# Two buffers in turn for the rows of the first attention's bias table

## The chip, the cores and the metric

The kernel runs on one core of one Trainium2 chip, as one launch. The metric is the device time of that launch in microseconds, and less is better. Five runs of the kernel before have a median of 1389.54 us (1382.15 to 1393.66).

## The reference, cut to what matters

The reference is a chain of four layers, each a half step of a feed-forward block, an attention, and another half step of feed-forward. The change lies in the first attention, whose scores get a bias that depends only on how far query and key lie apart, per head:

```python
x = x + 0.5 * _L0_ffn_ref(_layernorm(x, axis=-1), ...)
x = x + _L0_attn_ref(_layernorm(x, axis=-1), ..., L0_attn_rel_pos_emb)

# in _L0_attn_ref: x is (4, 512, 128), 16 heads of 8
att = jnp.einsum('bhtd,bhsd->bhts', q, k) / np.sqrt(D)
table = rel_pos_emb.reshape(2 * MAX_LEN - 1, H, D).sum(axis=-1)
pos = jnp.arange(T)
rel_idx = pos[:, None] - pos[None, :] + (MAX_LEN - 1)
bias = jnp.transpose(table[rel_idx], (2, 0, 1))
att = att + bias[None]
att = jnp.where(pos[None, :] > pos[:, None], -jnp.inf, att)
```

MAX_LEN is 128 and an index beyond the table is clamped to its last row, so a key more than 127 places back gets one constant per head.

## The kernel before, in words

Everything is 32-bit floating point. The 2048 tokens lie in four batches of 512 (`xs[b]`, 128 partitions by four tiles of 128). The first feed-forward is a mixture of eight experts, the class `Mixture`. Its method `experts` loops over the experts: `fetch` reads an expert's tokens from DRAM (`d_f<-disp_f`, L788), `prepare` transposes them (L807), then PE multiplies them by the two weights (L831, L867), VectorE adds the bias (L847), ScalarE weighs (L852), and GpSimd scatters the rows to a DRAM tensor `res_f` with indirect DMAs (L853). The last of these scatters ends the mixture.

The first attention, `l0_attn` (L1621), begins per batch with `combine` (L877): a read of that batch's rows of `res_f` (`r_f<-res_f`, L882, issued by SP), the addition to `xs[b]` (L883), a norm (L191 to L209), and PE's transposes (`T_a`, L218), from which queries, keys and values are made (L1535, L1463, L1396). Each score tile on VectorE then adds the bias table (`sc_a<-s_a,table`, L998 and L1002).

The table is made by the generator `prep_table` (L1553), whose steps are called in between other work. One row of 384 numbers per head (zeros, 128 biases, minus 1e30) goes to DRAM as `rows` (`tab_rows`, L1575). `fetch(h)` (L1581) reads for two heads the rows that are shifted by one element from partition to partition (`rev<-tab_rows`, 256 KB, L1583). A product with the matrix `flip` on PE (L1596, two passes of 128x512 each) turns the order of the partitions, and ScalarE copies the product into the table (`table<-turned`, L1597). There are 16 heads, hence eight reads, eight products and eight copies, named here by their first head: 0, 2, ... 14.

`behind_expert` (L2579) hands the steps out. The first reads are traced beside the fourth expert; the products and the other reads are traced after all eight experts (`whole(made)`, L2592) and ahead of `l0_attn`. The tile `rev` has the tag `raw` in the pool `stage`, which has five buffers for that tag. The same five serve other short-lived tiles, among them the raw weights that `load_T` reads (L166), so also those of the second layer (`prep_l1`, L1658: `raw_gate1T`, `raw_wg1T`, `raw_wu1T`, `raw_sg1T`, `raw_su1T`).

What sets the order: a planner that builds the program gives each engine and each DMA queue a static order and inserts the waits. Inside some stretches (`manual_schedule`) the order on the compute engines is that of the source; the stretch of the first attention is one (L1314: PE, VectorE, ScalarE, GpSimd, not SP). The experts and the table's products lie outside of them, and SP's queue of DMAs there is the planner's. A DMA in SP's queue that waits holds up those behind it.

## Time and profile before

| | |
|---|---|
| median of five runs | 1389.54 us |
| profiled execution, its own time | 1394.12 us |
| its span | 1392.4 us |
| mean granted clock of TensorE | 0.912 |
| PE busy | 1182.6 us (85%) |
| VectorE, ScalarE, GpSimd busy | 63%, 50%, 50% |
| products with `flip` on PE (L1596) | 92.7 to 100.8 us, 16 passes |
| reads `rev<-tab_rows` (L1583) | eight, issued 54.5 to 95.6 us |
| first use of the table on VectorE (L1002) | 116.6 us |

Times inside the execution count from the start of the span. PE is TensorE's matmuls, PEld its weight loads, DVE VectorE, ACT ScalarE, POOL GpSimd, and SPq the instructions with which SP issues DMAs. In a timeline a line gives start, duration, engine, line of the kernel, operation, output and inputs, and how many instructions are merged; the bracket at its end is the time that the engine sat idle before it, and what ended that. In the chain that ended last, a line gives start, duration and what held the chain in that time.

### The profile page before, as it was taken

To read this page: it belongs to the slowest core of one execution; us is meant where nothing else is said; L and a number is where in the kernel's file an instruction comes from. 1 tells how busy PE (TensorE), PEld (TensorE's weight loads), DVE (VectorE), ACT (ScalarE), POOL (GpSimd) and SP (SyncE) were. 2 spreads that over 40 slices of the span, in tenths; PEclk is the share of its full clock that TensorE was granted. 3 is DMA by queue.
4 is the path that set the end of the run, shared out by engine and by line. 5 is a ranking of instruction groups with operands and counts; after the bars stand their busy time and mean duration, and the time that the engine had idled before them with its cause. 6 is when DMAs were issued, how large, how long until landed. Compare 5 with 4: busy or idle time off the path is not lost.

```text
span 1392.4 us, 27536 instructions
## 1 busy us (share of the span) xinstructions
PE 1182.6 (85%) x9665; PEld 765.8 (55%) x9665; DVE 877.1 (63%) x3269; ACT 691.9 (50%) x1481; POOL 694.5 (50%) x786
## 2 busy tenths in 40 slices
PE   5787999996999999998989897649599999898494
PEld 4554776775766666666755453437354444343272
DVE  5236878772366557776549999724286787783253
ACT  3244977883443367776732221114236766565132
POOL 5545878882534767876624243344432334212253
PEclk9997999997999999999999997669778999998697
DMA  8533433203425584341039200032133313100334
GB/s 272 179 86 105 126 97 102 72 6 94 145 63 132 163 281 145 93 133 60 2 68 329 92 16 16 16 98 79 53 99 114 107 41 97 46 16 16 85 92 113
DMA packets 116649, 137.60 MB, mean 99 GB/s; under 512 B 11160, under 2 KB 68744, under 8 KB 116512
## 3 DMA queue, kind: packets, MB, share of 16 engines
q1 hardware_dynamic: 107456, 121.05, 29.1%
q0 software_dynamic: 6656, 13.22, 2.9%
q10 hardware_dynamic: 2400, 1.57, 0.4%
q8 instruction: 77, 1.26, 0.4%
q14 instruction: 60, 0.49, 0.1%
HBM read 78.22 MB, written 57.58 MB: 98 GB/s over the span
## 4 chain that ended last, share of the span: by engine, by line
PE 54%; DVE 22%; issue 9%; POOL 6%; DMA 5%; ACT 3%; another core or an unknown queue 1%; SPq 0%; POOLq 0%; DVEq 0%; ACTq 0%
PE t_a L1026 9%; PE s_a L968 6%; PE h_f L831 5%; PE acc_a L1048 5%; PE o_f L867 5%; PE acc_a L1215 4%; DVE top_a L1073 3%; DVE x L2279 3%; POOL res_f L853 2%; PE ot_a L1268 2%; PE t_a L968 2%; DVE sc_a L1002 1%; PE t_a L1103 1%; DVE sc_a L998 1%; DMA d_f<-disp_f 1%
## 5 line engine op out<-in xcount | busy, mean ns | idle before, releaser
L1013 POOL TENSOR_SCALAR sc_a<-sc_a,top_a 128x128 f32<-128x128 f32 (+3 forms) x256 | 275.9, 1093 | 74.2 <-DVE top_a L998 48.1
L968 PE MATMUL s_a<-k_a,q_a 32*128 32x512 f32 (+3 forms) x1040 | 183.3, 488 | 20.7 <-DVE top_a L1073 7.6
L1026 PE MATMUL t_a<-ident,sc_a 128*128 128x128 f32 x1280 | 174.3, 284 | 8.1 <-DVE top_a L1002 7.7
L1073 DVE TENSOR_REDUCE top_a<-s_a 128x1 f32<-128x512 f32 x240 | 150.9, 682 | 40.7 <-PE t_a L1103 18.6
L853 POOL DMA_INDIRECT res_f<-y_f,back_f x112 | 107.1, 956 | 127.2 <-ACT y_f L852 90.1
L1109 ACT ACTIVATE w_a<-t_a 128x512 f32<-128x512 f32 x240 | 127.8, 600 | 74.1 <-PE t_a L1103 39.6
L1026 PEld LDWEIGHTS t_a<-ident,sc_a 128*128 128x128 f32 x1280 | 145.8, 145 | 33.5 <-issue 12.6
L1015 ACT ACTIVATE sc_a<-sc_a,top_a 128x128 f32<-128x128 f32 (+3 forms) x256 | 134.2, 576 | 14.5 <-DVE top_a L1002 10.3
L1035 ACT ACTIVATE w_a<-t_a 128x256 f32<-128x256 f32 (+2 forms) x192 | 95.0, 528 | 64.4 <-PE t_a L1026 63.2
L968 PEld LDWEIGHTS s_a<-k_a,q_a 32*128 32x128 f32 x1040 | 79.5, 190 | 72.8 <-issue 26.3
L867 PE MATMUL o_f<-w_l,h_f 128*128 128x128 f32 (+1 forms) x896 | 110.6, 278 | 1.4 <-ACT h_f L835 0.9
L831 PE MATMUL h_f<-dT_f,w_l 128*128 128x320 f32 (+1 forms) x256 | 106.7, 555 | 2.6 <-ACT dT_f L809 2.6
L867 PEld LDWEIGHTS o_f<-w_l,h_f 128*128 128x128 f32 (+1 forms) x896 | 102.4, 184 | 10.4 <-DVE back_f L816 3.9
L1048 PE MATMUL acc_a<-w_a,vpad 128*32 128x128 f32 x2560 | 98.8, 280 | 0.6 <-ACT w_a L1035 0.6
L1037 ACT COPY w_a<-t_a 128x256 f32<-128x256 f32 (+2 forms) x192 | 93.6, 526 | 8.1 <-PE t_a L1026 7.8
L1002 DVE CUSTOM_DVE_ANT_0 sc_a<-s_a,future 128x128 f32<-128x128 f32 (+3 forms) x128 | 62.3, 487 | 49.0 <-PE s_a L968 40.8
L852 ACT ACTIVATE y_f<-o_f,d_f 128x128 f32<-128x128 f32 (+1 forms) x112 | 39.0, 394 | 102.7 <-DVE o_f L847 90.4
L1215 PE MATMUL acc_a<-w_a,vpad 128*32 128x256 f32 x1024 | 87.7, 413 | 2.4 <-ACT w_a L1109 2.3
L1048 PEld LDWEIGHTS acc_a<-w_a,vpad 128*32 128x32 f32 x2560 | 63.4, 110 | 23.5 <-issue 18.2
L968 PE MATMUL t_a<-q_a,k_a 32*128 32x512 f32 x240 | 73.4, 516 | 1.1 <-DVE top_a L1073 0.5
L836 DVE TENSOR_SCALAR h_f<-h_f,b1T_l 128x320 f32<-128x320 f32 (+1 forms) x64 | 41.4, 650 | 51.9 <-PE h_f L831 47.4
L807 PE MATMUL dT_f<-ident,d_f 128*128 128x128 f32 (+1 forms) x112 | 21.2, 296 | 58.3 <-DMA d_f<-disp_f 39.8
(607 smaller groups left out, 2297.9 us busy)
## 6 DMA issues: line engine op xcount, KB each, us to landing
fac_a<-fac_a_sb SPq DMA_DIRECT2D x36, 256.0 KB
d_f<-disp_f SPq DMA_DIRECT2D x32, 260.0 KB
w_l<-in_L_ffn_w_dram SPq DMA_DIRECT2D x16, 512.0 KB
cb_f<-rows_f SPq DMA_DIRECT2D x16, 512.0 KB
q_a<-fac_a SPq DMA_DIRECT2D x32, 256.0 KB
k_a<-fac_a SPq DMA_DIRECT2D x32, 256.0 KB
disp_f<-zeros_f SPq DMA_DIRECT2D x4, 2048.0 KB
q_a<-qrows_a SPq DMA_DIRECT2D x30, 256.0 KB
```

Source lines behind the costliest of these rows:

```text
L831: nc.tensor.matmul(ps[u][:, :cap], w1[:, e, (c + u) * P : (c + u + 1) * P], dT, start=True, stop=True)
L853: nc.gpsimd.indirect_dma_start(out=self.back[e * per + s][:, :], out_offset=bass.IndirectOffsetOnAxis(ap=back[:m, s : s + 1], axis=0), in_ ...
L867: nc.tensor.matmul(po[:m, s, :], h[:, c, s * P : s * P + m], w2[:, e, c, :], start=(c == 0), stop=(c == NC - 1),)
L968: nc.tensor.matmul(ps[:, n0:n1], q[r : r + SLOT, i * P : (i + 1) * P].bitcast(as_), k[r : r + SLOT, n0:n1].bitcast(as_), start=True, stop= ...
L1013: nc.gpsimd.tensor_scalar(sc, sc, top, None, ALU.subtract)
L1015: nc.scalar.activation(sc, sc, AF.Exp, bias=top, scale=-1.0)
L1026: nc.tensor.transpose(ps[:, x * n + j * P : x * n + (j + 1) * P], st["sc", u, i, r0 + x][:, j * P : (j + 1) * P], ident,)
L1035: nc.scalar.activation(w[:, :m], ps[:, :m], AF.Exp)
L1048: nc.tensor.matmul(st["acc", u][r * SLOT : (r + 1) * SLOT, i * P : (i + 1) * P], vpads[b % 2][:, j, g * 4 + r, :], st["w", u, i, r][:, j * ...
L1073: nc.vector.tensor_reduce(st["top", u][:, i, r : r + 1], ps, AX.X, ALU.max, negate=True)
L1109: nc.scalar.activation(w, st["t", u, j, r], AF.Exp)
L1215: nc.tensor.matmul(acc[r * SLOT : (r + 1) * SLOT, n0:n1], vpads[b % 2][:, j, g * 4 + r, :], st["w", u, j, r, half] if ("w", u, j, r, half) ...
```

## The change

`fetch` makes a new tile only for the first two pairs of heads (h = 0 and 2). Every later pair is read into the tile of the pair two before it, which the product of that pair must have read first. Two reads instead of three are traced ahead of the products, and each product is followed by the read for two products further on instead of three.

```diff
         def fetch(h):
-            revs[h] = stage.tile([P, 2, 2 * P], FP, name=f"rev{h}", tag="raw")
+            if h < 4:
+                revs[h] = stage.tile([P, 2, 2 * P], FP, name=f"rev{h}", tag="raw")
+            else:
+                revs[h] = revs[h - 4]
             nc.sync.dma_start(
                 revs[h],
                 bass.AP(tensor=rows.tensor, offset=rows.offset + h * 3 * P, ap=[[1, P], [3 * P, 2], [1, 2 * P]]),
...
-        for h in range(0, 6, 2):
+        for h in range(0, 4, 2):
             fetch(h)
         yield
         for h in range(0, NH, 2):
             ps = bank(f"turned{h}")
             nc.tensor.matmul(ps, flip, revs[h].rearrange("p h s -> p (h s)"), start=True, stop=True)
             nc.scalar.copy(by_head[:, h : h + 2, P:], ps.rearrange("p (h s) -> p h s", h=2))
-            if h + 6 < NH:
-                fetch(h + 6)
+            if h + 4 < NH:
+                fetch(h + 4)
```

## The prediction

> **What bounds the kernel now.** I read the page first, then the chain of waits around the change, then SP's queue and PE's rows there, then how long reads take elsewhere. The page says what the whole is worth:

> ```profile
> PE 1182.6 (85%) x9665; PEld 765.8 (55%) x9665; DVE 877.1 (63%) x3269; ACT 691.9 (50%) x1481; POOL 694.5 (50%) x786
> PE 54%; DVE 22%; issue 9%; POOL 6%; DMA 5%; ACT 3%; another core or an unknown queue 1%; SPq 0%; POOLq 0%; DVEq 0%; ACTq 0%
> ```

> PE is busy for 85% and carries 54% of the chain, and DMA only 5%. But the eight products run once, at 92.7 to 100.8 us, in a seam between the first mixture's experts and the first attention, and there the chain is this:

> ```profile
> 93.49 0.96 POOL res_f L853
> 94.75 4.11 DMA res_f<-y_f,back_f
> ...
> 99.04 2.93 DMA r_f<-res_f
> 101.97 0.02 issue
> 101.99 0.70 DVE x L883
> ...
> 105.90 1.13 DVE n_a L209 x4
> ```

> The experts' last scatter is sent, lands at 98.86, its result is read back (`r_f`, L882), added, normalized, and only then PE transposes it. No product stands in this chain. SP's queue shows who stands beside it:

> ```profile
> 54.52 2.56 SPq L1583 DMA_DIRECT2D rev<-tab_rows  x5
> 60.63 0.36 SPq L788 DMA_DIRECT2D d_f<-disp_f  x1
> 61.04 0.64 SPq L1422 DMA_DIRECT2D br_l<-in_L_attn_b_qkv_dram  x2
> 66.40 11.90 SPq L788 DMA_DIRECT2D d_f<-disp_f  x3
> 93.89 2.08 SPq L1583 DMA_DIRECT2D rev<-tab_rows  x3
> 99.04 0.36 SPq L882 DMA_DIRECT2D r_f<-res_f  x1
> 99.51 0.34 SPq L167 DMA_DIRECT2D raw_gate1T<-n_L_ffn_gate_weight_dram  x1
> ```

> Five reads are in early, since five buffers carry the tag; the other three go at 93.89, 94.75 and 95.61, each 0.01 to 0.02 us after the product that frees its buffer (ACT's copies, which start at a product's end, begin at 93.90, 94.75, 95.61). Then comes `r_f`, the read that the chain needs, in the same queue. PE around it:

> ```profile
> 92.73 5.72 PE L1596 MATMUL turned<-rev,flip 128*128 128x512 f32 x12
> 98.82 1.96 PE L1596 MATMUL turned<-rev,flip 128*128 128x512 f32 x4 [0.36 <-DMA rev<-tab_rows]
> 106.39 1.15 PE L218 MATMUL T_a<-ident,n_a 128*128 128x128 f32 x4 [5.62 <-DVE n_a L209]
> ```

> Products end at 100.8 and PE then waits 5.62 us for DVE. That is the slack the change can eat.

> **Removed, and nearly free.** Three reads fewer are ahead at 54.5 (five become two). Three buffers stay free there, so the weight loads of the next layer (`raw_gate1T` and its followers, issued 99.51 to 102.56, first used at 324.1) can go early: 4 + 256 + 256 KB instead of 768 KB in the same place. The next `d_f` read has slack, so I take zero; its cover is the expert work on PE until 92.7, and if it came 2.6 us later (512 KB at the 200 GB/s of 95 to 98.8 us) it would still be within the 3.2 us between a `d_f` landing (60.63 + 2.63) and its transposes at 66.46. The loads themselves are 220 us early either way. Eight products, eight copies of 586 ns and eight reads remain as many as before.

> **Added: two chains of read and product.** Read 4 must now wait for product 0, read 6 for product 2, and so on: three links in each chain. A link is L (SP's issue until the product can start) plus a product. A product after a wait takes 1.15 us (92.73 to 93.88), one behind another 0.86 (93.88 to 94.73). L is the uncertain term. The same read with two more behind it took 93.89 to 97.33, 3.44 us; the next, among three, 94.75 to 98.79, 4.04; an undisturbed 256 KB read of `read<-res_f` after the second mixture took 2.62. With two in flight, not three, I am nearest to the first row, a little below it: L = 3.2, ends 2.62 and 4.04. From product ends 93.88 and 94.73:

> - reads 4 and 6 land at 97.1 and 97.95; products end at 98.25 and 99.1
> - reads 8 and 10 land at 101.5 and 102.3; products end at 102.6 and 103.5
> - reads 12 and 14 land at 105.8 and 106.7; products end at 107.0 and 107.9

> PE does the products in order ahead of T_a (L218), which wanted to start at 106.39: 1.5 us late. With L = 2.62 the last product ends at 106.1, before T_a wants to start; with 4.04 at 110.35, 4.0 late. ACT's last copy ends 0.6 us behind the last product, at 108.5, before ACT's next work (110.50), and the first use of the table on DVE is at 116.62: both free at L = 3.2, and their cover moves along with T_a if L is longer.

> [...]

> **Moved on SP.** Six reads, not three, now queue near `r_f`. Where it stands among them is fixed when the program is built. The rows of before tell how: five `rev` reads are issued at 54.5 though the source has two of them behind products of 92.7, and `raw_gate1T`, from behind the whole attention, directly follows `r_f`. So the queue goes by expected readiness, and `r_f` was expected between the frees of the third and the fourth product, 1.7 to 2.6 us behind the first one's. Read 8 is ready a link later than read 4 (at least 2.62 + 1.15 = 3.8 us). So I expect read 4, read 6, `r_f`, read 8. Then `r_f` doesn't wait for a product, but read 8 (ready 98.25) waits behind `r_f` for the scatter. Against that, the scatter should land sooner: its 4.11 us stand in the 768 KB of three reads; the same scatter ahead of `read<-res_f` took 2.13 (the chain at 389.68). With 512 KB in its way I put it half way, landing near 98. Then read 8 goes at about 98.5, some 0.3 later than reckoned, and T_a's own inputs are ready about 0.9 earlier, which doesn't count while PE is held until 107.9. Net +1.5 us. Bounds: -0.3 (L = 2.62: products end at 106.1, T_a's inputs are there before) and +4.0.

> **Sum.** The profiled execution took 1394.12 us (span 1392.4 and 1.7 around it): +1.5 gives 1395.6. It lay 4.6 above the median of the five runs (1389.54); the step is the same, so the median goes to 1391.0, 0.1% up. About 0.5% (7 us) is what a measurement of this kernel can tell from no change.

> **Rivals.**
> - *`r_f` behind all six reads on SP* (slower). Then read 14 goes at the end of product 10, 103.5, and `r_f` one issue later (0.47 us, as 99.04 to 99.51): 104.0 instead of 99.04, +4.9 us, and T_a, add and norm all shift; the products end before and hide nothing. With L = 2.62 it is +3.7, with 4.04 +6.6. For it: the reads come first in the source. Against it: the readiness argument above. It decides as soon as one read that waits for a product of the second pair stands ahead of `r_f`.
> - *T_a ahead of the last products on PE* (no change or faster). T_a was ready at 106.4 and products 12 and 14 start at 105.8 at the earliest, so an expectation a little different turns their order. Then the scatter's earlier landing counts: 4.11 down to 2.13 at best, -1.9 us; at worst 0.5 for the products in front of L1535 (108.42). Against it: in before all products stand ahead although PE was idle.
> - *Another static order elsewhere.* The order of SP and of the engines outside the hand-written stretches is made anew, with three buffers free for 50 us. I can't read a price for it here; the chain shows what a read out of turn costs: `d_f` 4.81 and 4.43 us at 918 and 948, against 2.63 at 40.58. Two such reads more, less the usual length, are 4 us, four are 9; as much could go away, since such reads are in the chain already.
> - *The change doesn't bite*: not possible for the order of reads, since each buffer is rewritten; only its cost can be hidden, and that is the lower end of my forecast.

> **How the numbers follow.** Forecast 0.50 (+1.5, from -0.3 to +4.0); `r_f` behind the reads 0.22 (+3.7 to +6.6); T_a ahead 0.12 (-1.9 to +0.5); another order 0.16 (-4 to +9). The five runs of before have a standard deviation of 4.4 us; a median of five has about 0.56 of it, and a difference of two such medians 1.4 times that, 3.5 us. That puts 0.07, 0.35, 0.02 and 0.60 of the four cases above +7 us: 0.035 + 0.077 + 0.002 + 0.096 = 0.21. Below -7 us it is 0.03, 0.01, 0.12 and 0.30 of them: 0.015 + 0.002 + 0.014 + 0.048 = 0.08. Same: 0.71. The range goes from 1385 (forecast's low end less the looseness) to 1398 (the reads ahead of `r_f`, and a little): about 1 in 10 is left out on either side.

> **What would show it.** Right: two `rev` issues near 54.5; six `rev` issues from 93.9 on, `r_f` the third or fourth behind the second pair's free; products in four pairs with idle PE of about 2 us between, released by the DMA; T_a waiting for PE's own products and starting near 107.9; the scatter's landing shorter than 4.11. Wrong: `r_f` issued after 102 (the first rival), L outside 2.6 to 4.1, T_a among the products, or a difference of more than 3 us that doesn't lie between 92 and 110 us.

## The result, and the profile after

The kernel with two buffers takes 1393.73 us (median of 27 runs, 1388.04 to 1400.86) against 1387.68 us (median of 53 runs, 1381.28 to 1395.37) for the kernel before on the same chip. The ratio is 1.0043, with a 95% interval of 1.0030 to 1.0056: slower by 6.0 us. (Ratios are estimated from all runs of both kernels, so they can differ a little from the quotient of the medians.) The direction was forecast and the time lies in the range of 1385 to 1398; the loss was forecast as 1.5 us, from -0.3 to +4.0, and is four times that.

The profiled execution took 1400.42 us (span 1398.7, mean granted clock 0.906), 6.3 more than the one of before (1394.12; span 1392.4, clock 0.912). Every line number behind the edit is 3 higher: the products are L1599, the reads L1586, the copies L1600.

First, is it all in the seam? A good mark is SP's first read of the second mixture's result, `read<-res_f`, which starts when the whole first attention and that mixture are through. Lines of the timeline of SP give start, duration, line and count; before, then after:

```profile
391.96 2.02 SPq L2622 DMA_DIRECT2D read<-res_f  x4
```

```profile
398.35 2.02 SPq L2625 DMA_DIRECT2D read<-res_f  x4
```

That is 6.39 us later, and from there to the end of the span it is 1000.4 us in both (1392.4 - 391.96 and 1398.7 - 398.35). So in this pair of profiles the loss arises ahead of 398 us. (That the rest agrees to 0.1 us is in part chance: over other profiles it varies by 12 us, as the last experiments show.) Of the 6.39, 1.06 us is there before the first product starts (92.73 against 93.79), and 1.05 of that already at 54 us, ahead of the first instruction that the change moves; before, then after:

```profile
54.10 0.38 SPq L788 DMA_DIRECT2D d_f<-disp_f  x1
```

```profile
55.15 0.38 SPq L788 DMA_DIRECT2D d_f<-disp_f  x1
```

So this part is not the change's, and 5.3 us arise behind it. PE's timeline of after in the seam, with the idle time ahead of a row and what ended it in the bracket:

```profile
93.79 1.99 PE L1599 MATMUL turned<-rev,flip 128*128 128x512 f32 x4
98.05 3.67 PE L1599 MATMUL turned<-rev,flip 128*128 128x512 f32 x4 [2.28 <-DMA rev<-tab_rows]
104.20 3.00 PE L1599 MATMUL turned<-rev,flip 128*128 128x512 f32 x4 [2.49 <-DMA rev<-tab_rows]
109.06 2.05 PE L1599 MATMUL turned<-rev,flip 128*128 128x512 f32 x2 [1.86 <-DMA rev<-tab_rows]
111.76 2.05 PE L1599 MATMUL turned<-rev,flip 128*128 128x512 f32 x2 [0.65 <-DMA rev<-tab_rows]
113.60 1.06 PE L218 MATMUL T_a<-ident,n_a 128*128 128x128 f32 x4
115.54 1.95 PE L1535 MATMUL qk_a<-nT_a,w_l 128*128 128x512 f32 x4 [0.88 <-DVE nT_a L157]
```

From the first product to `T_a` (called the way from here on) it takes 113.60 - 93.79 = 19.81 us; before it was 106.39 - 92.73 = 13.66. The 6.15 us between them can be read off PE's rows alone:

| us on PE in the way | before | after |
|---|---|---|
| rows of products | 5.72 + 1.96 = 7.68 | 1.99 + 3.67 + 3.00 + 2.05 + 2.05 = 12.76 |
| idle among them, ended by a read | 0.36 | 2.28 + 2.49 + 1.86 + 0.65 = 7.28 |
| idle ahead of `T_a`, ended by VectorE | 5.62 | 0 |
| less what the modelled ends overlap | 0 | 0.23 |
| sum | 13.66 | 19.81 |

The idle time among the products is what the prediction spoke of. It grew by 6.92 us, and the slack of 5.62 ate most of that. The other term was not in the sum at all: **the same sixteen passes are busy for 5.08 us longer.** The windows of after say why (their columns: stretch, its length, then busy time and instructions of PE, PEld, DVE, ACT and POOL, then the granted TensorE clock, the share of the DMA engines and GB/s):

```profile
98.00:100.00 2.00, 1.95 (x3) 0.78 (x4) 0.00 (x0) 0.00 (x0) 0.00 (x0) 0.55 0.25 66
...
106.00:108.00 2.00, 1.20 (x2) 0.00 (x0) 1.12 (x4) 0.71 (x2) 0.77 (x2) 0.50 0.58 113
...
116.00:118.00 2.00, 2.00 (x6) 0.95 (x5) 0.57 (x2) 0.69 (x1) 0.44 (x1) 1.00 0.00 0
```

The first pair (94 to 96 us) runs at a granted 1.00. After the first gap the clock is 0.55, and in the windows where products run it stays between 0.50 and 0.76 until the attention is under way. A product that took 0.86 to 1.15 us takes 1.7 to 2.1, but for product 8 with 1.33, most of which lies ahead of a fall of the clock at 105.03.

A gap of 2.28 us was enough to lower the clock, and the trace shows why. Cut where the clock changes, it falls into stretches of 3.41 us, each wholly at 1.00 or at 0.50:

```profile
94.79:98.20 3.41, 1.13 (x4) 0.30 (x3) 0.00 (x0) 1.17 (x2) 1.62 (x2) 1.00 0.63 176
98.20:101.62 3.42, 3.42 (x4) 0.77 (x4) 0.00 (x0) 0.59 (x1) 0.00 (x0) 0.50 0.24 76
101.62:105.03 3.41, 0.92 (x3) 0.40 (x3) 2.25 (x9) 0.59 (x1) 0.05 (x1) 1.00 0.59 182
105.03:108.44 3.41, 2.17 (x3) 0.46 (x2) 1.12 (x4) 1.17 (x2) 2.10 (x3) 0.50 0.48 109
```

The clock fell at the end of stretches in which PE was busy for 1.13 and for 0.92 us, and neither was wholly idle. In the traces of before and after every change of the clock lies a whole number of such stretches behind the one ahead of it; worked out from windows of 2 us, the clock was low for some 3.4 and 6.8 us with half of the products moved, and for 6.8 with eight buffers. Between the first product and the first scores, the clock fell behind stretches at full clock with at most 1.50 us of PE work (1.50 with the later reads on ScalarE, below, 107.68 to 111.09) and stayed up behind those with 1.53 us (two buffers with PE kept busy, below), 1.57 (before, 99.20 to 102.61) or more. It came back behind those with 2.80 us (after, 111.86 to 115.27) or more, and stayed low behind those with 2.17 us (before, 106.02 to 109.44) or less; with three buffers it stayed low behind some 2.7 too, an estimate from the rows there. So in these traces not the gap alone decides, but how much work shares a stretch with it. This is read from the seam only: in the attention, with its short products, the clock fell behind fuller stretches too (before: 3.11 us of work from 116.26 to 119.67).

What held the end, by the chain of waits of after (start, duration, what):

```profile
95.81 3.92 DMA res_f<-y_f,back_f
...
100.32 3.84 DMA rev<-tab_rows
...
104.20 3.01 PE turned L1599 x4
...
107.23 4.39 DMA rev<-tab_rows
...
111.76 2.05 PE turned L1599 x2
113.81 0.87 PE T_a L218 x4
```

In before, the chain went from the scatter through `r_f`, the sum and the norm. Now it goes from the scatter through SP's order (read 8 behind `r_f`) into the reads and products. SP's queue of after is the one that was forecast, two reads early, then 4, 6, `r_f`, 8:

```profile
55.58 1.02 SPq L1586 DMA_DIRECT2D rev<-tab_rows  x2
...
94.94 1.22 SPq L1586 DMA_DIRECT2D rev<-tab_rows  x2
99.82 0.36 SPq L882 DMA_DIRECT2D r_f<-res_f  x1
100.32 5.57 SPq L1586 DMA_DIRECT2D rev<-tab_rows  x3
105.94 0.46 SPq L882 DMA_DIRECT2D r_f<-res_f  x1
107.23 0.36 SPq L1586 DMA_DIRECT2D rev<-tab_rows  x1
```

Part of the loss comes back: L1535 takes 1.95 us where it took 3.75 before. Before, PE had waited 5.62 us ahead of `T_a`, and it was `T_a` and L1535 that ran at the low clock (granted 0.50 from 106 to 108 and from 110 to 112). In after the clock is back at 1.00 by then (115.27). From the first product to the first scores (L968) it is 22.4 us before (115.11 - 92.73) and 27.0 after (120.76 - 93.79): 4.6 more. At `read<-res_f` the difference is 5.3.

### The profile page after: what moved, and what is told of

It reads as the page before. It is cut to its first block, busy times and chain, and to the rows that moved or that the text cites. A ratio compares the mean times of both kernels' runs of the same rounds, so it can differ in the third digit from the quotient of the medians.

```text
span 1398.7 us, 27536 instructions
## 1 busy us (share of the span) xinstructions
PE 1191.7 (85%) x9665; PEld 769.9 (55%) x9665; DVE 877.9 (63%) x3269; ACT 691.7 (49%) x1481; POOL 694.7 (50%) x786
## 3 DMA queue, kind: packets, MB, share of 16 engines
q10 hardware_dynamic: 2400, 1.57, 0.4%
## 4 chain that ended last, share of the span: by engine, by line
PE 61%; DVE 19%; issue 6%; POOL 5%; DMA 4%; ACT 3%; another core or an unknown queue 1%; SPq 0%; POOLq 0%; DVEq 0%; ACTq 0%
PE t_a L1026 9%; PE h_f L831 7%; PE o_f L867 7%; PE s_a L968 6%; PE acc_a L1048 5%; PE acc_a L1215 4%; DVE top_a L1073 3%; DVE x L2282 2%; PE ot_a L1268 2%; PE t_a L968 2%; PE t_a L1103 1%; DVE sc_a L1002 1%; PE y_f L2271 1%; DVE sc_a L998 1%; PE lg_f L1711 1%
## 5 line engine op out<-in xcount | busy, mean ns | idle before, releaser
L968 PE MATMUL s_a<-k_a,q_a 32*128 32x512 f32 (+3 forms) x1040 | 182.5, 487 | 21.5 <-DVE top_a L1073 7.1
L853 POOL DMA_INDIRECT res_f<-y_f,back_f x112 | 107.1, 957 | 128.3 <-ACT y_f L852 91.4
L968 PEld LDWEIGHTS s_a<-k_a,q_a 32*128 32x128 f32 x1040 | 79.2, 189 | 73.6 <-issue 24.5
L867 PEld LDWEIGHTS o_f<-w_l,h_f 128*128 128x128 f32 (+1 forms) x896 | 102.6, 184 | 10.7 <-DVE back_f L816 3.9
L1048 PEld LDWEIGHTS acc_a<-w_a,vpad 128*32 128x32 f32 x2560 | 63.5, 110 | 23.3 <-issue 17.9
L968 PE MATMUL t_a<-q_a,k_a 32*128 32x512 f32 x240 | 73.7, 524 | 0.5 <-DVE top_a L1073 0.5
```

What stands on the lines that cost most here:

```text
L853: nc.gpsimd.indirect_dma_start(out=self.back[e * per + s][:, :], out_offset=bass.IndirectOffsetOnAxis(ap=back[:m, s : s + 1], axis=0), in_ ...
L867: nc.tensor.matmul(po[:m, s, :], h[:, c, s * P : s * P + m], w2[:, e, c, :], start=(c == 0), stop=(c == NC - 1),)
L968: nc.tensor.matmul(ps[:, n0:n1], q[r : r + SLOT, i * P : (i + 1) * P].bitcast(as_), k[r : r + SLOT, n0:n1].bitcast(as_), start=True, stop= ...
L1048: nc.tensor.matmul(st["acc", u][r * SLOT : (r + 1) * SLOT, i * P : (i + 1) * P], vpads[b % 2][:, j, g * 4 + r, :], st["w", u, i, r][:, j * ...
```

## The experiments

Two theories were set against each other. *Clock*: PE's waits lower its clock, so a link of the chain costs a read and a product at about 2.1 us. *Latency*: the links are longer only because reads land late, and the products' longer rows cost little. Ratios are against the kernel before on the same chip. The first four kernels shared one (before there: 1362.2 us, median of 26), the last four another (before: 1390.29, median of 35). "The way" is again first product to `T_a`: 13.66 in before, 19.81 in after, from the two profiles above. The kernel before has a profile from the chip of the result only, so ways are compared across chips.

### One buffer

```diff
-            if h < 4:
+            if h < 2:
                 revs[h] = stage.tile(...)
             else:
-                revs[h] = revs[h - 4]
+                revs[h] = revs[h - 2]
...
-        for h in range(0, 4, 2):
+        for h in range(0, 2, 2):
             fetch(h)
...
-            if h + 4 < NH:
-                fetch(h + 4)
+            if h + 2 < NH:
+                fetch(h + 2)
```

> One buffer instead of two: seven links of read and product in one chain, all in front of T_a. Measure: from the start of the first product to the start of T_a (L218); 13.7 us in the kernel before, 19.8 in the changed one. Clock theory (PE waits for reads, its granted clock falls to a half, and a product then costs 2.0 us or so instead of 1.15): a link is 3.2 + 2.0 = 5.2, T_a at 1.15 + 7 x 5.2 = 37.6 us, +24 us against before. Latency theory (only the reads' landing counts, products cost 1.15): a link is 4.35, T_a at 31.6, +18 us. If the loss is not the chain of links, it stays near +6.

Measured: 1387.17 us, ratio 1.0190 (1.0173 to 1.0206), 25 us slower. PE's timeline:

```profile
94.23 1.85 PE L1599 MATMUL turned<-rev,flip 128*128 128x512 f32 x2 [3.17 <-DMA rev<-tab_rows]
99.19 2.08 PE L1599 MATMUL turned<-rev,flip 128*128 128x512 f32 x2 [3.11 <-DMA rev<-tab_rows]
```

The way is 127.97 - 89.94 = 38.0 us, 24.4 more than in before, and the whole kernel lost as much. No two reads of the table travel together here, and from the fifth read on (106.98) no `r_f` is near them either. Two of these four on the chain of waits:

```profile
106.98 3.04 DMA rev<-tab_rows
...
112.17 3.27 DMA rev<-tab_rows
```

A read by itself lands in 3.04 to 3.27 us, which is the prediction's L of 3.2. (The read at 101.29, with an `r_f` sent 0.4 us behind it, took 3.54.) A product after such a wait costs 2.04 to 2.08 from the third on, not 1.15. The clock theory's 37.6 is met and latency's 31.6 is not.

### Three buffers

```diff
-            if h < 4:
+            if h < 6:
...
-                revs[h] = revs[h - 4]
+                revs[h] = revs[h - 6]
...
-        for h in range(0, 4, 2):
+        for h in range(0, 6, 2):
...
-            if h + 4 < NH:
-                fetch(h + 4)
+            if h + 6 < NH:
+                fetch(h + 6)
```

> Three buffers: only two rounds of waiting, of which the first starts 0.86 us later. Clock theory: products 6 to 14 run at half clock; the last ends some 13 us after the first one's start, just ahead of T_a's own inputs at 13.7, so 0 to +0.5 us against before. Latency theory: the last ends at about 11, no loss. Both: not the +6 of two buffers.

Measured: 1362.24 us, ratio 1.0004 (0.9989 to 1.0019): no difference from before, which has five buffers for these tiles. The way is 103.97 - 89.25 = 14.7 us. Its last two products still come late, and slow, at 3.75 us for the pair:

```profile
100.43 3.75 PE L1599 MATMUL turned<-rev,flip 128*128 128x512 f32 x4 [3.25 <-DMA rev<-tab_rows]
```

The last product ends 14.9 us after the first one's start, where the clock theory had 13 and latency 11; the read that it waits for, sent 0.5 us behind an `r_f`, took 4.62:

```profile
95.67 4.62 DMA rev<-tab_rows
```

`T_a` starts at 103.97 as they end, about a microsecond later than before's way would have put it. So two links in each chain still fit the slack, but for about a microsecond that the total does not show, and the third one of two buffers does not. Having the reads follow the products is not the loss as such.

### Two buffers, with PE kept busy

The kernel after, with two unused products of the finished part of the table after each of the first three pairs. They fill PE's idle time with work that nobody waits for.

```diff
             if h + 4 < NH:
                 fetch(h + 4)
+            if h % 4 == 2 and h < 12:
+                for w in (h - 2, h):
+                    nc.tensor.matmul(
+                        bank(f"warm{w}"), flip, by_head[:, w : w + 2, P:], start=True, stop=True
+                    )
```

> The changed kernel with two more products of 512 columns after each of the first three pairs, which read table columns that are finished and whose result nobody uses, so that PE doesn't idle while the next pair is read. Clock theory: the granted clock stays near 1, products cost 0.86 to 1.15 us, the way from the first product to T_a falls from 19.8 to about 16.2 us, and the loss against before from 6 to about 2.5 us. Latency theory: the way stays at 19.8 and the loss at 6, or grows where the added products are in the way.

Measured: 1365.68 us, ratio 1.0027 (1.0014 to 1.0040), 3.5 us slower than before; the way is 107.85 - 89.99 = 17.9 us.

```profile
100.55 1.95 PE L1599 MATMUL turned<-rev,flip 128*128 128x512 f32 x4 [1.88 <-DMA rev<-tab_rows]
102.34 1.97 PE L1605 MATMUL warm<-table,flip 128*128 128x512 f32 x4
...
106.92 1.09 PE L1599 MATMUL turned<-rev,flip 128*128 128x512 f32 x2 [0.51 <-DMA rev<-tab_rows]
```

The granted clock is 1.00 in every stretch from 90 to 108 us, the emptiest of them too:

```profile
98.04:101.45 3.41, 1.53 (x4) 0.48 (x3) 2.25 (x9) 0.00 (x0) 0.33 (x2) 1.00 0.52 149
```

The products are back at 0.9 to 1.2 us. The four that stand on the path (products 4, 8, 10 and 14) cost 4.34 us together against 7.16 in after: 2.8 us are the clock's. The way fell by 1.9 only, between the two theories' 16.2 and 19.8. Reads 4 and 8 took 0.7 us longer than in after, and the `r_f`s held reads up on SP for 0.4 us more; read 14 took 0.3 less. Read 8 and read 14 on the chain of waits:

```profile
96.38 4.03 DMA rev<-tab_rows
...
102.67 4.12 DMA rev<-tab_rows
```

So the clock is shown to be a cause in the way. The total moved with it, from 6.0 us over before to 3.5, but on another chip and with intervals that overlap (1.0030 to 1.0056, 1.0014 to 1.0040). What is left of the way over before's is the reads that the products wait for.

### Half of the products moved into the attention

The kernel after, with the first four products where they are and the other four called step by step inside the attention, behind the first scores (at 126 and 135 us in the trace).

```diff
-        for h in range(0, NH, 2):
+        def product(h):
             ps = bank(f"turned{h}")
...
+        for h in range(0, 8, 2):
+            product(h)
         l0["table"] = biases
         yield
+        for h in range(8, NH, 2):
+            product(h)
+            if h == 10:
+                yield
...
-        whole(made)
+        next(made)
...
-        l0_attn(f00.combine, lambda _: (), lambda b: (
+        l0_attn(f00.combine, lambda _: made, lambda b: (
```

> The changed kernel with the last four products handed to the first attention, which does them beside its second and third unit; only the first four stand in front of T_a. Both theories of the chain: T_a starts when its own inputs are there (13.7 us after the first product or, with the scatter landing sooner, up to 1.5 earlier), the +6 in front of it is gone, and PE pays up to 4 x 0.86 = 3.4 us within the attention: 0 to +3.4 us against before. If the loss comes from anything but products standing in front of T_a (the weights that are loaded earlier, the reads left on SP), it stays near +6.

Measured: 1367.34 us, ratio 1.0034 (1.0023 to 1.0044), 5.1 us slower than before, worse than the expected 0 to 3.4. So the total alone does not tell this from the other case that the expectation names, a loss near +6 that has nothing to do with products ahead of `T_a`; the trace does. The seam did as forecast: the way is 102.74 - 89.79 = 12.95 us, shorter than before's, and `T_a` waits for VectorE again:

```profile
102.74 1.25 PE L218 MATMUL T_a<-ident,n_a 128*128 128x128 f32 x4 [4.74 <-DVE n_a L209]
```

The four products reappear on the chain of waits inside the attention:

```profile
126.47 2.91 PE turned L1599 x4
...
135.35 1.91 PE turned L1599 x4
```

Here PE is the bound, so every pass is paid in full, 4.8 us in all, the first pair mostly at a granted clock of 0.50 (126 to 128 us), some 3 us behind a wait of 5.70 us for a DMA. Between the first scores and the mark `read<-res_f` lie 277.2 us, against 273.7 in the profile with three buffers on the same chip, so most of it is still there. How the total comes to 5.1 is not traced further. For this work the seam is the better place: PE has idle time there, and the question is how much fits.

### The later reads on another queue

The kernel after, with its last six reads issued by ScalarE, so that read 8 does not stand behind `r_f` on SP.

```diff
-            nc.sync.dma_start(
+            (nc.sync if h < 4 else nc.scalar).dma_start(
                 revs[h],
```

> The changed kernel with the six later reads issued by ScalarE's queue, each behind its copy, so that neither `r_f` stands between them on SP. If the place on SP makes the loss, read 8 goes 0.3 us earlier and read 14 lands in 3.1 to 3.3 us instead of 4.5: the way from the first product to T_a falls from 19.8 by 1.5 to 2 us. If the landing is long because other reads share the 16 DMA engines, whichever queue issued them, the way stays within 1 us of 19.8 and the time near +6. The granted clock stays at 0.5 to 0.6 among the products in both.

Measured: 1395.38 us, ratio 1.0039 (1.0017 to 1.0061), 5.1 us slower than before; the way is 113.54 - 94.16 = 19.4 us. `r_f` and its follower went together as soon as the scatter had landed (100.08 and 100.49), read 8 went at the end of product 4, and little was won. Reads 8 and 14 on the chain of waits:

```profile
100.08 4.44 DMA rev<-tab_rows
...
108.12 3.44 DMA rev<-tab_rows
```

Read 8, sent with the first `r_f`, took 4.44 us (3.84 in after); read 14, now with read 12 alone ahead of it, 3.44 (4.39). So the place in SP's queue is not the cause of the long landings. They go with what else was sent shortly before, whichever queue issued it.

It also shows that a wait does not always lower PE's clock:

```profile
98.86 2.13 PE L1599 MATMUL turned<-rev,flip 128*128 128x512 f32 x4 [2.72 <-DMA rev<-tab_rows]
104.57 3.52 PE L1599 MATMUL turned<-rev,flip 128*128 128x512 f32 x4 [3.57 <-DMA rev<-tab_rows]
```

Behind 2.72 us of idle time the pair ran at 1.00, behind 3.57 at 0.57. In after 2.28 us had sufficed for 0.55. The expectation had the low clock in all later products, and that part failed. The stretches of 3.41 us explain it:

```profile
94.03:97.44 3.41, 2.11 (x6) 0.68 (x4) 0.28 (x1) 1.81 (x4) 2.44 (x3) 1.00 0.21 63
97.44:100.85 3.41, 1.99 (x4) 0.59 (x4) 0.00 (x0) 0.59 (x1) 0.00 (x0) 1.00 0.43 139
100.85:104.27 3.42, 0.14 (x1) 0.00 (x0) 0.00 (x0) 0.59 (x1) 0.00 (x0) 1.00 0.79 216
104.27:107.68 3.41, 3.11 (x4) 1.13 (x4) 2.24 (x9) 0.59 (x1) 0.35 (x2) 0.50 0.27 91
```

The gap of 2.72 us (96.14 to 98.86) is split between two stretches with 2.11 and 1.99 us of work; the one of 3.57 us fills a stretch but for 0.14. The stretches do not start with the kernel's own work: one begins 1.00 us behind the first product in after (94.79 against 93.79) and 0.13 us ahead of it here (94.03 against 94.16). So where a gap falls on them differs between these two kernels; whether it differs between runs of one kernel is not shown, since each has one trace here.

### The kernel before, with PE kept busy ahead of `T_a`

If a low clock costs time in the seam, before pays it too, at `T_a` and L1535. Five unused products behind the last one fill its wait.

```diff
+        for w in range(5):
+            nc.tensor.matmul(
+                bank(f"warm{w}"), flip, by_head[:, NH - 2 : NH, P:], start=True, stop=True
+            )
```

> The kernel before with five more products of 512 columns behind the last one, reading finished table columns, result unused, in the 5.6 us in which PE waits for `r_f` and the norm. Clock theory: T_a and the first products of queries and keys, which ran at a granted 0.50, run near 1: T_a 0.6 instead of 1.15 us, the first two passes of L1535 1.1 instead of 2.06; from the first product to the first scores (L968) 20.8 instead of 22.4 us, and the time 1.5 us less. Latency theory: nothing changes, or it is slower where the added products stand in T_a's way.

Measured: 1389.45 us, ratio 1.0007 (0.9989 to 1.0026), no difference. In the seam it did what was expected, but for `T_a`, which took 1.01 us and not 0.6:

```profile
102.66 4.56 PE L1601 MATMUL warm<-table,flip 128*128 128x512 f32 x10 [0.68 <-ACT table L1597]
...
109.14 1.95 PE L1535 MATMUL qk_a<-nT_a,w_l 128*128 128x512 f32 x4 [0.88 <-DVE nT_a L157]
```

L1535 takes 1.95 us, not 3.75, and from the first product to the first scores it is 20.3 us (114.45 - 94.17), not 22.4. The total did not follow.

### Eight buffers, all reads beside the experts

The other direction of the change: a pool of their own for the eight reads, open during the first experts only, so that no read is left for the seam.

```diff
-            revs[h] = stage.tile([P, 2, 2 * P], FP, name=f"rev{h}", tag="raw")
+            revs[h] = rev_pool[0].tile([P, 2, 2 * P], FP, name=f"rev{h}", tag="rev", bufs=8)
...
-        for h in range(0, 6, 2):
+        for h in range(0, NH, 2):
             fetch(h)
...
-            if h + 6 < NH:
-                fetch(h + 6)
...
-        f00.experts(l0["w"], lambda _: next(beside, None))
-        whole(made)
+        with tc.tile_pool(name="revs", bufs=1) as rp:
+            rev_pool.append(rp)
+            f00.experts(l0["w"], lambda _: next(beside, None))
+            whole(made)
```

> A buffer for each of the eight reads, in a pool that is open for the first mixture's experts only, all read beside them. No product waits and no read stands near the last scatter. If the late reads hold up that scatter, it lands in 2.2 us instead of 4.1, `r_f` goes 1.9 us sooner, T_a starts 11.8 us after the first product instead of 13.7, and the time is 1.9 us less than before. If the scatter is long for another reason, nothing changes.

Measured: 1391.65 us, ratio 1.0008 (0.9986 to 1.0030), no difference. The chain of waits shows the scatter without reads beside it:

```profile
95.92 2.13 DMA res_f<-y_f,back_f
```

2.13 us against 4.11 in before and 3.92 in after: the reads in the seam do delay the scatter, and two reads beside it delay it almost as much as three. (With one buffer, so with one read beside it, `r_f` was issued 2.77 us after the scatter, against 2.31 us here and 4.01 in after.) The way is 105.42 - 93.90 = 11.5 us, 2.1 less than before.

### Both of these

Eight buffers and the five unused products together (the two edits above in one kernel).

> Eight buffers and the five added products behind the last one. If both theories hold, both gains add: T_a 11.8 us after the first product, the first scores (L968) at 18.9 instead of 22.4, and the time 3.4 us (0.25%) less than before. Where the five added products last longer than the wait, T_a is late by the rest, up to 1.2 us, and the gain is 2.2.

Measured: 1390.05 us, ratio 0.9990 (0.9972 to 1.0008). The seam is as short as expected, 19.0 us from the first product to the first scores (112.72 - 93.72) against 22.4; the 3.4 us in the total are at the edge of the interval, and the result is inconclusive.

Why the last three do not show in the total can be read in part from the mark at `read<-res_f`. From the first product to there it is 299.2 us in before (391.96 - 92.73), 296.8 with PE kept busy (390.92 - 94.17), 297.7 with eight buffers (391.59 - 93.90) and 297.2 with both (390.89 - 93.72): 1.5 to 2.5 us are still there after 300 us, in one profile each. Behind the mark, the rest of the span is 1000.4, 990.7, 1000.6 and 1002.9 us in these four profiles. It varies by 12 us without any edit there, so a gain of 2 us (0.15%) is under what these runs resolve, and none of the three is claimed as faster.

## Why the prediction was right or wrong

**The range held by its width.** The forecast proper, +1.5 us with bounds of -0.3 and +4.0, did not contain the 6.0 us. The range of 1385 to 1398 did, because it was widened for the noise of medians of five and for the first rival, and that rival's mechanism did not occur. The time falling inside is luck in that sense; the order of events was forecast, the size was not.

**The order on SP: right.** Reads 4 and 6, then `r_f`, then read 8, as argued from expected readiness. The second `r_f` came in ahead of read 14, which was not foreseen; it was issued 1.3 us before that read and travelled with it. What a wait on SP does to those behind it shows in before: product 6 had freed its buffer at 96.47, and `raw_gate1T`, next in turn for one, went at 99.51 behind `r_f`, which waited for the scatter until 98.86.

**`r_f` not held up: right.** It went at 99.82, 0.09 us after the scatter had landed (95.81 + 3.92), and the first rival (behind all six reads, +3.7 to +6.6) fell, though its size is what was measured.

**Products ahead of `T_a` on PE: right.** The second rival (`T_a` among them) fell too.

**The freed buffers: no cost seen.** `raw_gate1T` and the next two loads moved to 56.7 to 57.6 us, as forecast (the last two of the five went at 111.14 and 113.84). Their cost in the experts was taken as zero, and the profile agrees: of the 1.06 us by which the first product started later, 1.05 were there ahead of them. The kernel of three buffers, which frees two of the five, gives a bound on such effects: it differs from before by 0 (-1.5 to +2.6 us).

**Another static order elsewhere: absent.** VectorE, ScalarE and GpSimd run through the same instructions in the same order in both traces, PE too up to 1000 us, and SP's queue differs only in these reads, the first two `r_f` and the moved loads. The third rival fell.

**The scatter sooner: wrong, and of little consequence.** It landed in 3.92 us, not about 3: two reads beside it cost nearly as much as three. Had it landed in 3, `r_f` would have been issued before product 4 ended, and read 8 would not have waited 0.27 us behind it. `T_a`'s inputs were nevertheless ready first, as forecast.

**The step that failed is the price of a link.** From the end of product 0 to that of product 14 the forecast had 13.9 us: three reads at 3.2, with products at 1.15, 1.15, 0.86 and 1.15. After took 18.9 (94.95 to 113.85). The difference of 5.0 splits by term (a read lasts from its issue, or from the end of the product that frees its buffer, to its product's first weight load on PE; a product ends where ACT's copy of it starts):

| term | forecast | measured | more |
|---|---|---|---|
| product 4 | 1.15 | 2.00 | 0.85 |
| product 8 | 1.15 | 1.33 | 0.18 |
| product 10 | 0.86 | 1.71 | 0.85 |
| product 14 | 1.15 | 2.12 | 0.97 |
| read 4 | 3.2 | 3.11 | -0.09 |
| SP, read 8 behind `r_f` | 0 | 0.27 | 0.27 |
| read 8 | 3.2 | 3.88 | 0.68 |
| read 14 | 3.2 | 4.50 | 1.30 |

- *Products, 2.85 us.* They were priced from rows of before in which PE came straight out of the experts at full clock (granted 1.00 from 92.37 to 95.78). The row of 1.15 us (92.73 to 93.88), which the prediction calls a product after a wait, had no wait ahead of it: PE had worked until 92.80. The change itself takes that away, since it puts 2 us of idle time ahead of each pair. The prediction named those gaps and did not ask what clock they leave. The kernel of before had shown the answer: L1535, behind a wait of 5.62 us, takes 3.75 us there. The kernel with PE kept busy confirms the term (2.8 us on the path).
- *Reads, with the wait on SP, 2.16 us.* L = 3.2 is right for a read alone (3.04 to 3.27 with one buffer) and for read 4, which had company behind it only. Read 8, sent 0.5 us behind `r_f`, took 3.88, and read 14, which sets the end, sent with read 12 and the second `r_f` less than 2 us ahead of it, 4.50. That is over the upper bound of 4.04, and over the 4.1 that the prediction named as a sign of being wrong. The kernel with the later reads on ScalarE moved the long landing from read 14 to read 8 along with the company, which speaks for the company and against the place on SP. The 0.3 us that read 8 would wait behind `r_f` were named in the prediction but left out of its net +1.5; they came to 0.27.

Some readings behind the sum were loose as well. The 2.62 us that stand for an undisturbed read belong to the first of four reads sent in 2.02 us. The rate from 95 to 98.8 us, taken as 200 GB/s, is 228 in the trace, which changes nothing. The reads of the table took 3.04 to 3.27 us alone, not 2.62.

The gaps among the products alone would not have made the loss: their growth (6.92 us) was mostly covered by the slack (5.62), and what made up 6 was the slower work behind them.

**Still open:** how the landing of a read depends on each of its neighbours (only their presence was varied here), and whether the seam's shorter forms are worth their 2 us in the total.

## What to carry to other kernels

When a change puts a wait between matmuls, price the wait and the matmuls behind it: here the same product cost 0.9 to 1.15 us out of running work and 1.7 to 2.1 behind most of the waits of 2 to 4 us, and up to `T_a` that was more than half of the surprise. Ask how much work PE has in any 3.4 us (in the seam its clock fell behind stretches of 3.41 us with 1.50 us or less), not only how long one gap is. Work that lies in an engine's slack is free only as a whole: once the last link of a chain of read and product reaches past the slack, every further link costs its whole price (two, three or seven links in a row, for three buffers, two or one: 0, +6, +25 us). Take a DMA's duration from a row with the same company; the same read took 3.1 us alone and 4.5 among others.
